# Handing the last rows of a row scan to the column scan tile to tile, with stores by quarter and loads on two queues

## The chip, the core and the metric

The kernel runs on one core of a Trainium2 chip. The metric is the device time of one execution in microseconds (us). Three executions of the kernel before took 4289.52, 4292.32 and 4297.63 us; the median is 4292.32.

## What is computed

Two layers run one after the other on a tensor of 32 images x 48 channels x 64 rows x 128 columns in float32. A layer normalizes its input by groups of three channels (`_gn`), runs four recurrences over the picture, and adds the result to its input. Each recurrence takes one row, or one column, after the other: the new one is the input plus a convolution of the one before (48 to 48 channels, 5 taps along the row or column, and a bias).

```python
def step(w, b):
    def f(carry, inp):
        nxt = inp + _conv1d(carry, w, b)
        return (nxt, nxt)
    return f
_, d_rest = jax.lax.scan(step(down_w, down_b), d0, xs[1:])     # down the 64 rows
_, u_rest = jax.lax.scan(step(down_w, down_b), u0, seq)        # and up again
_, r_rest = jax.lax.scan(step(right_w, right_b), r0, ws[1:])   # right over the 128 columns
_, l_rest = jax.lax.scan(step(left_w, left_b), l0, R[Ww - 2::-1])  # and left again
...
x = x + _L0_conv_ref(_gn(x), L0_conv_down_w, ...)
x = x + _L1_conv_ref(_gn(x), L1_conv_down_w, ...)
```

No step can begin before the one ahead of it has ended. The column scans need every row of the finished row scans.

## The kernel before

**Phases.** Images are taken in four groups of eight. `PHASES` (L104) lists twelve phases in their order: a `rows` phase scans one group down and up (126 steps), a `cols` phase scans a pair of groups right and left (254 steps). `scans` (L802) yields the steps; `step` (L728) is nine matmuls on TensorE (L741) and three additions on VectorE (L750), one for each of three blocks of 128 partitions, in the order 0, 2, 1.

**Layouts.** A row tile holds 384 partition rows (3 blocks `o` of 128): eight columns `e` of an octet times 48 channels. Its free axis runs over the row `h` and then over the 16 octets and the 8 images. `PIECES` (L51) says where the 48 channels of each `e` lie; channels of e = 2 and e = 5 straddle two blocks. A column tile is laid out the other way: `e` on the partitions is the row modulo 8, and the free axis runs over half (which group of the pair), octet of rows `a`, column modulo 8, octet of columns and image. The 128 columns are held by quarters of 32; a quarter is a third of the arena (`quarter`, L630), and the fourth takes the place of the first, which is spilled to DRAM (`spill_unit`).

**Going from rows to columns** is done through DRAM. `move_rows` (L589) stores rows of the row tile to the DRAM tensor `ups` in pieces of 128 bytes, ten DMAs for up to eight rows. `load_unit` (L633) loads one block of one half of a quarter, three or four DMAs.

**Order of work.** Work beside the scans is put on an agenda: `at(t, fn, ...)` (L820) runs `fn` when t steps have been written, and `in_order` (L235) chains all instructions of an engine in the order in which they were written. DMAs are issued from three queues: SP (`nc.sync`, the default of `dma`, L230), ACT (`nc.scalar`) and POOL (`nc.gpsimd`). A queue issues in order, so a DMA that waits holds up all that are behind it.

**The seam.** Twice a `cols` phase directly follows the `rows` phase of its second group (`follows`, L883): phase 2 after phase 1, and phase 6 after phase 5. There is no other work between, so the column scan must wait for the last rows. `plan_rows` (L853) stores the rows of the upward scan as they are finished, by eights (SP), but cuts the last eight in two: rows 2 to 7 when row 2 is done and rows 0 and 1 at the end. In `plan_cols` (L888) the second half of quarter 0 is loaded from POOL: rows 32 to 63, 16 to 31 and 8 to 15 ahead of the seam, then rows 2 to 7, and at the end rows 0 and 1. `hold_queues` (L648) puts a small DMA to the DRAM tensor `pin` on SP and a small copy on ACT, both reading what the first column step wrote. So the loads of quarter 1 behind them (L907; half 0 on SP, half 1 on ACT) start after that step. Quarter 2 (L910), the spill (L911) and quarter 3 (L912) follow on SP. During phase 2 SP also reads the rows of the next group (`plan_input`, L833): `take_in` loads them, ACT takes their statistics, POOL permutes them and SP stores them, each piece behind the one before.

Of the kernel before, what the change touches and what calls it, by code (L numbers as in the profile page):

```python
# [29 lines left out]
F32 = mybir.dt.float32  # L30
# [13 lines left out]
E8 = 8  # L44
FULL = 128
NG = E8 * C // FULL
NQ = 4
# [73 lines left out]
def kernel(  # L121
# [79 lines left out]
        dram.tile([2 * NG, FULL, UNIT], F32, tag=f"spill{i}", name=f"spill{i}")  # L201
        for i in range(4)
    ]
    pin = dram.tile([FULL, 1], F32, tag="pin", name="pin")


    HELD = (2, 1, 0)
# [3 lines left out]
        for half in range(2)  # L211
    }

    def by_row(t, e, h0, h1):


        t = t.rearrange("c (i q a e n) -> e a c i q n", i=E8, q=NQ, a=NH, e=E8)[e, h0 // E8]
        return t[:, h0 % E8 : h0 % E8 + h1 - h0].rearrange("c i q n -> c (i q) n")

    def lines(t, h0, h1):  # L220

# [8 lines left out]
    def dma(dst, src, queue=None):  # L230
        (queue or nc.sync).dma_start(dst, src)

    tail = {}

    def in_order(fn, *args):  # L235


        traced = nc.cur_bb.bb.instructions
        n = len(traced)
        fn(*args)  # L240
        for ins in traced[n:]:
            if ins.engine in tail:
                tc.add_manual_dep(
                    ins,
                    tail[ins.engine].name,
                    mybir.DependencyInfo(
                        mybir.DependencyClass.NoSync, mybir.DependencyReason.DATA
                    ),
                    reason="in_order",
                )  # L250
            tail[ins.engine] = ins

    def pieces(o):
# [332 lines left out]
    def row(k, h):  # L586
        return row_views(k)[h // HALF][:, :, h % HALF]

    def move_rows(k, h0, h1, to_dram):  # L589

        _, layer, g = PHASES[k]
        view = row_views(k)[h0 // HALF]
        t = (ups if to_dram else source)[layer][g]
        for h in range(h0, h1, E8):
            end = min(h1, h + E8)
            for o in range(NG):
                for e, c0, c1, p0 in pieces(o):
                    here = view[p0 : p0 + c1 - c0, o, h % HALF : h % HALF + end - h]
                    here = here.rearrange("p h (q n) -> p (h q) n", q=NQ)
                    there = by_row(t, e, h, end)[c0:c1]  # L600
                    if to_dram:
                        dma(there, here)
                    else:
                        dma(here, there)
# [25 lines left out]
    def quarter(k, j):  # L630
        return slot[slots(k)[j % 3]].rearrange("p (o s n) -> p s o n", s=2, o=NG)
# [13 lines left out]
                queue,  # L645
            )

    def hold_queues(k):  # L648

        done = quarter(k, 0)[:, 0, 0, RUN : RUN + 1]  # L650
        dma(pin, done)
        nc.scalar.copy(junk[:, BN - 1 :], done)

    def spill_unit(k, i, back):
        _, layer, pair = PHASES[k]
# [197 lines left out]
    def plan_rows(k, t0, prev):  # L853
        if k == 1:
            ahead, scaled = (-34, -18, -3, 12), (-12, -2, 17, 33)
        elif prev == "cols":
            ahead, scaled = (-28, -12, 4, 20), (-13, 3, 19, 35)
        else:
            ahead, scaled = (-54, -43, 0, 11), (-22, -8, 16, 30)
        if k:  # L860
            for i in range(4):
                at(t0 + ahead[i], move_rows, k, i * LOAD, (i + 1) * LOAD, False)
                at(t0 + scaled[i], scale_rows, k, i * LOAD, (i + 1) * LOAD)

        cuts = list(range(0, H + 1, E8))
        following = PHASES[k + 1][0] == "cols"
        if following and follows(k + 1):
            cuts = [0, E8 // 4] + cuts[1:]
        for h0, h1 in zip(cuts, cuts[1:]):
            t = t0 + 2 * (H - 1) - h0  # L870
            if k == 0:
                t += 16 if h0 >= HALF else 68
            elif not following:
                t = t0 + 92 + 5 * (H - h1) / E8 + (34 if h1 <= HALF else 0)
            at(t, move_rows, k, h0, h1, True)
        at(
            t0 + H - 1,
            nc.gpsimd.tensor_copy,
            last.rearrange("p (o n) -> p o n", o=NG),
            row(k, H - 1),  # L880
        )
# [6 lines left out]
    def plan_cols(k, t0, prev):  # L888
        _, layer, pair = PHASES[k]
        n = 2 * NG  # L890
        after = prev == "cols"
        if follows(k):
            at(t0 + 1.2, hold_queues, k)
        for i in range(n):
            if follows(k) and UNITS[i][1] == 1:
                other = nc.gpsimd
                at(t0 - 31 + i, load_unit, k, 0, i, 4, NH, 0, E8, other)
                at(t0 - 13 + i, load_unit, k, 0, i, 2, 4, 0, E8, other)
                at(t0 - 6 + i / n, load_unit, k, 0, i, 1, 2, 0, E8, other)
                at(t0 - 1.5, load_unit, k, 0, i, 0, 1, E8 // 4, E8, other)  # L900
                at(t0, load_unit, k, 0, i, 0, 1, 0, E8 // 4, other)
            else:
                early = 30 if after else 46 if k == 2 else 70
                at(t0 - early + 2 * i, load_unit, k, 0, i)
            if follows(k):
                queue = nc.scalar if i % 2 else nc.sync
                at(t0 + 1.5, load_unit, k, 1, i, 0, NH, 0, E8, queue)  # L907
            else:
                at(t0 + (3 if after else -24 + 2 * i), load_unit, k, 1, i)
            at(t0 + (38 if after else 8) + 2 * i, load_unit, k, 2, i)  # L910
            at(t0 + 33 + 2 * i, spill_unit, k, i, False)  # L911
            at(t0 + 50 + 2 * i, load_unit, k, 3, i)  # L912
        final = k == len(PHASES) - 1
        left = t0 + W - 1
        end = left + W - 1
        for i in range(n):

            t = left + 64 + 2 * i if layer == 0 else left + 39.5 + 4.5 * i
            at(t, spill_unit, k, i, True)
        units = []  # L920
        for n_done, j in enumerate((3, 2, 1, 0)):
            every = 4.5
            if j == 0 and PHASES[k + 1 if not final else k][0] == "rows":
                every = 7
            units += [(left + 34 + 32 * n_done + every * i, j, i) for i in range(n)]
        stats = None
        if layer == 0:
            stats = ResultStatsV(f"r{2 * pair}"), ResultStatsA(f"r{2 * pair + 1}")
        tiles = [stage[:, i] for i in range(4)]
        if layer:  # L930
            tiles += spare_tiles[0 : 2 if final else 1]
        n = len(tiles)
        direct = [u for u in units if not (final and u[1] == 0)]

        for u, (t, j, i) in enumerate(direct):
            nat = tiles[u % n]
            o, half = UNITS[i]
            if u < n:
                at(left + 16, load_residual, k, j, i, nat)
            if layer == 0:  # L940
                if u >= n:
                    at(direct[u - n][0] + 3, load_residual, k, j, i, nat)
                at(t, add_residual, k, j, i, nat)
                at(t + 4, keep_result, k, j, i)
                unit = quarter(k, j)[:, half, o]
                if half == 0:
                    for b in range(GB):
                        at(t + 5 + b, stats[0].take, j, o, unit, b)
                else:
                    at(t + 1, stats[1].take, j, o, unit)  # L950
            else:

                at(t, add_residual, k, j, i, nat)
                at(t + 2.5, permute_unit, k, j, i, nat, (nc.gpsimd, nc.scalar, nc.scalar))
                if final or j not in HELD:
                    at(t + 4.5, store_result, k, j, i, nat)
                else:
                    at(t + 4.5, hold_result, j, i, nat)
                if final and j == 1:
                    at(t + 4.7, load_residual, k, 0, i, last_tiles(k)[i])  # L960

                if u >= 2 and u - 2 + n < len(direct):
                    at(t + 4.6, load_residual, k, *direct[u - 2 + n][1:], tiles[(u - 2) % n])
        if layer == 0:
            t = units[-1][0] + 14
            g = 2 * pair
            spread(t, scaling(f"r{g}", 1, g, stats[0], r_masks, 8), 1)
            spread(t + 20, scaling(f"r{g + 1}", 1, g + 1, stats[1], r_masks, 8), 1)
        if layer:

            at(left + 10, nc.scalar.copy, junk[:, BN - 1 :], quarter(k, 3)[:, 0, 0, RUN - 1 : RUN])
        if layer and not final:
            todo = [(j, half, e) for j in HELD for half in range(2) for e in range(E8)]
            for n, what in enumerate(todo):
                at(end + 63 + 1.9 * n, let_result, *what)
        if final:
            at(end + 4, last_results, k)
# [231 lines left out]
```

## Time and profile before

| | before |
|---|---|
| median of three executions | 4292.32 us |
| the profiled execution | 4290.3 us |
| its span, first to last instruction | 4288.2 us |
| TensorE busy (matmuls) | 4058.9 us, 95% |
| VectorE busy | 2164.5 us, 50% |
| ScalarE busy | 1340.1 us, 31% |
| GpSimd busy | 886.2 us, 21% |
| granted TensorE clock, mean | 0.981 |
| DMA | 680.12 MB in 2,116,733 packets, 2,005,440 of them under 512 bytes |

Times in the trace count from the start of the span. In the lists of engines PE is TensorE, PEld its weight loads, DVE is VectorE, ACT ScalarE, POOL GpSimd and SP SyncE; "SPq" and "ACTq" are DMAs that these issue. `step_00r` is a step of layer 0, pair 0, right; `step_00d` and `step_00u` are layer 0, group 0, down and up. `arena<-upa` is a load from the DRAM tensor `ups` of layer 0, `upa<-arena` a store to it. "[14.10 <-DMA ...]" at the end of a line is how long the engine had been idle ahead of it and what ended that. fp32 matmuls show as two records each, so a step has 18 of them.

### The profile page before, as it was taken

To read this page: it belongs to the slowest core of one execution; us is meant where nothing else is said; L and a number is where in the kernel's file an instruction comes from. 1 tells how busy PE (TensorE), PEld (TensorE's weight loads), DVE (VectorE), ACT (ScalarE), POOL (GpSimd) and SP (SyncE) were. 2 spreads that over 40 slices of the span, in tenths; PEclk is the share of its full clock that TensorE was granted. 3 is DMA by queue.
4 is the path that set the end of the run, shared out by engine and by line. 5 is a ranking of instruction groups with operands and counts; after the bars stand their busy time and mean duration, and the time that the engine had idled before them with its cause. 6 is when DMAs were issued, how large, how long until landed. Compare 5 with 4: busy or idle time off the path is not lost. (4 is left out here: it accounts for less than half of the span.)

```text
span 4288.2 us, 89979 instructions
## 1 busy us (share of the span) xinstructions
PE 4058.9 (95%) x36648; PEld 4029.3 (94%) x36648; DVE 2164.5 (50%) x6503; ACT 1340.1 (31%) x2662; POOL 886.2 (21%) x906
## 2 busy tenths in 40 slices
PE   3699998999999999998999999999999999999992
PEld 1699998999999999998999999999999999999992
DVE  6345444446664444444446654444444444444443
ACT  1584301435793564100006772613000002210122
POOL 4271001325323020010005310000000024510352
PEclk9899999999999999999999999999999999999996
DMA  9599799857998979679308979939289049999999
GB/s 213 113 216 162 105 167 168 245 127 213 230 198 156 163 140 160 103 127 206 85 1 242 222 154 149 148 50 161 43 140 200 1 78 247 247 243 156 180 202 182
DMA packets 2116733, 680.12 MB, mean 159 GB/s; under 512 B 2005440, under 2 KB 2056160, under 8 KB 2076384
## 3 DMA queue, kind: packets, MB, share of 16 engines
q1 hardware_dynamic: 2015904, 581.64, 70.2%
q10 hardware_dynamic: 97216, 86.44, 9.9%
q0 software_dynamic: 3200, 6.30, 0.5%
q8 instruction: 288, 4.72, 0.5%
q14 instruction: 125, 1.02, 0.1%
HBM read 397.38 MB, written 295.98 MB: 162 GB/s over the span
## 5 line engine op out<-in xcount | busy, mean ns | idle before, releaser
L614 ACT ACTIVATE arena<-arena,offset,scale 128x256 f32<-128x256 f32 (+2 forms) x816 | 575.6, 801 | 432.9 <-DMA arena<-mid 176.1
L673 POOL TENSOR_TENSOR arena<-arena 128x2048 f32<-128x2048 f32 x80 | 363.1, 4553 | 1386.0 <-PE step_10l L741 434.1
L569 POOL COPY arena<-arena 96x256 f32<-96x256 f32 x448 | 265.0, 650 | 553.8 <-DMA arena<-in_x 444.2
L512 ACT ACTIVATE early<-arena 128x256 f32<-128x256 f32 x192 | 129.4, 674 | 477.2 <-POOL arena L673 471.2
L741 PE MATMUL step_00r<-arena,early 128*128 128x128 f32 x2286 | 251.5, 274 | 14.1 <-DMA arena<-upa 14.1
L741 PEld LDWEIGHTS step_00r<-arena,early 128*128 128x128 f32 x2286 | 251.1, 185 | 14.5 <-issue 14.4
L741 PE MATMUL step_01r<-arena,early 128*128 128x128 f32 x2286 | 250.6, 273 | 14.4 <-DMA arena<-upa 14.4
L741 PEld LDWEIGHTS step_01r<-arena,early 128*128 128x128 f32 x2286 | 250.4, 185 | 14.6 <-issue 14.5
L741 PE MATMUL step_11r<-arena,early 128*128 128x128 f32 x2286 | 251.3, 273 | 8.2 <-DVE arena L750 8.2
L741 PEld LDWEIGHTS step_11r<-arena,early 128*128 128x128 f32 x2286 | 250.8, 185 | 8.7 <-DVE arena L750 8.6
L741 PE MATMUL step_00l<-arena,wleft 128*128 128x128 f32 x2286 | 249.1, 272 | 0.0
L741 PEld LDWEIGHTS step_00l<-arena,wleft 128*128 128x128 f32 x2286 | 248.6, 184 | 0.0
L741 PE MATMUL step_10l<-arena,wleft 128*128 128x128 f32 x2286 | 248.5, 272 | 0.0
L741 PE MATMUL step_11l<-arena,wleft 128*128 128x128 f32 x2286 | 248.5, 272 | 0.0
L741 PE MATMUL step_01l<-arena,wleft 128*128 128x128 f32 x2286 | 248.4, 272 | 0.0
L741 PE MATMUL step_10r<-arena,early 128*128 128x128 f32 x2286 | 248.4, 272 | 0.0
L741 PEld LDWEIGHTS step_10l<-arena,wleft 128*128 128x128 f32 x2286 | 248.4, 184 | 0.0
L741 PEld LDWEIGHTS step_11l<-arena,wleft 128*128 128x128 f32 x2286 | 248.4, 184 | 0.0
L741 PEld LDWEIGHTS step_01l<-arena,wleft 128*128 128x128 f32 x2286 | 248.4, 184 | 0.0
L741 PEld LDWEIGHTS step_10r<-arena,early 128*128 128x128 f32 x2286 | 248.4, 184 | 0.0
L698 ACT COPY arena<-arena 128x256 f32<-128x256 f32 x172 | 99.7, 656 | 411.5 <-POOL arena L673 162.2
L240 ACT COPY early<-arena 128x1 f32<-128x1 f32 x2 | 0.4, 191 | 657.9 <-DVE arena L750 657.9
(189 smaller groups left out, 7171.3 us busy)
## 6 DMA issues: line engine op xcount, KB each, us to landing
arena<-in_x SPq DMA_DIRECT2D x24, 1536.0 KB, 11.6
xin<-arena SPq DMA_DIRECT2D x96, 384.0 KB, 4.7
arena<-xin SPq DMA_DIRECT2D x96, 384.0 KB, 8.5
mid<-arena SPq DMA_DIRECT2D x96, 384.0 KB, 7.8
arena<-mid SPq DMA_DIRECT2D x192, 192.0 KB, 4.2
upb<-arena SPq DMA_DIRECT2D x192, 192.0 KB, 3.9
arena<-upb SPq DMA_DIRECT2D x96, 384.0 KB, 12.3
arena<-xin SPq DMA_DIRECT2D x186, 192.0 KB, 4.3
```

Source lines behind the costliest of these rows:

```text
L240: fn(*args)
L512: nc.scalar.activation(junk[:, 0:n], view[:, b], AF.Identity, accum_out=self.sum[:, i, j : j + 1])
L569: copy(dst[:, r, q], src[:, r0 + r, q])
L614: nc.scalar.activation(args[0], args[0], AF.Identity, bias=args[2], scale=args[1])
L673: eng.tensor_tensor(unit, unit, nat, ALU.add)
L698: copy(by_w(perm)[:, a], src[:, a])
L741: nc.tensor.matmul(part(whole(ps[o])[0:m], -s), weights[:, i, at : at + m], part(src(i), s), start=seen[o] == 1, stop=seen[o] == left[o],)
```

## The change

- **Sends.** At a seam the last eight rows no longer go through DRAM for the first quarter of the columns. A new `send_row` copies a row piece by piece from the row tile straight into quarter 0 of the column tile: one DMA for each run of channels that is contiguous on both sides, at most 48 partitions x 128 bytes. For e = 0 to 3 of every octet of columns it is called as each row is finished (47 DMAs in all for rows 7 to 0). For e = 4 to 7, `send_rest` does all eight rows after the last one (47 more). The DMAs alternate between ACT and SP. `in_order` chains them across the two queues where they are written (the chain orders their scheduling; it adds no wait on the chip).
- **Removed loads and stores.** The stores of rows 2 to 7 and 0 to 1 ahead of the columns, and the POOL loads of those rows, are gone.
- **Stores by quarter.** Rows 8 to 15 are stored at row 8 for quarter 0 alone. Quarter 1 of rows 0 to 15 is stored after the last row, and quarters 2 and 3 of them a step or two later (SP; 20 DMAs for each quarter).
- **Quarter 1.** Its loads change sides: half 0 goes on ACT, half 1 on SP. On SP they stand between the stores of quarter 1 and those of quarters 2 and 3.
- **Hold.** `hold_queue` keeps only the copy on ACT. The DMA to `pin`, and `pin`, are gone.

```diff
-    pin = dram.tile([FULL, 1], F32, tag="pin", name="pin")
...
+            if ins.engine in queues and "DMA" in ins.opcode:
+                if fn in together and "queue" in tail:
+                    tc.add_manual_dep(
+                        ins,
+                        tail["queue"].name,
...
+                tail["queue"] = ins
...
-    def move_rows(k, h0, h1, to_dram):
+    def move_rows(k, h0, h1, to_dram, q=None):
...
-                    here = here.rearrange("p h (q n) -> p (h q) n", q=NQ)
-                    there = by_row(t, e, h, end)[c0:c1]
+                    there = by_row(t, e, h, end, q)[c0:c1]
+                    if q is None:
+                        here = here.rearrange("p h (q n) -> p (h q) n", q=NQ)
+                    else:
+                        here = here[:, :, q * RUN : (q + 1) * RUN]
...
-    def hold_queues(k):
-
-        done = quarter(k, 0)[:, 0, 0, RUN : RUN + 1]
-        dma(pin, done)
-        nc.scalar.copy(junk[:, BN - 1 :], done)
+    turns = [0]
+
+    def send_row(k, h, wanted):
+
+        here = row(k - 1, h)
+        for e, c0, c1, o, p0 in PIECES:
+            if e not in wanted:
+                continue
+            for i, d0, d1, to, q0 in PIECES:
+                a, b = max(c0, d0), min(c1, d1)
+                if i != h or a >= b:
+                    continue
+                turns[0] += 1
+                dma(
+                    quarter(k, 0)[q0 + a - d0 : q0 + b - d0, 1, to, e * RUN : (e + 1) * RUN],
+                    here[p0 + a - c0 : p0 + b - c0, o, 0:RUN],
+                    nc.scalar if turns[0] % 2 else nc.sync,
+                )
+
+    def send_rest(k, wanted):
+
+        for e in wanted:
+            for h in range(E8 - 1, -1, -1):
+                send_row(k, h, (e,))
+
+    together += [send_row, send_rest]
+
+    def hold_queue(k):
+
+        nc.scalar.copy(junk[:, BN - 1 :], quarter(k, 0)[:, 0, 0, RUN : RUN + 1])
...
-        if following and follows(k + 1):
-            cuts = [0, E8 // 4] + cuts[1:]
+        seam = following and follows(k + 1)
+        if seam:
+            cuts = cuts[2:]
+            end = t0 + 2 * (H - 1)
+            at(end - E8, move_rows, k, E8, 2 * E8, True, 0)
+            for h in range(E8 - 1, -1, -1):
+                at(end - h, send_row, k + 1, h, range(0, E8 // 2))
+            at(end, send_rest, k + 1, range(E8 // 2, E8))
+            for q in range(1, NQ):
+                at(end + 0.1 if q == 1 else end + 1.6, move_rows, k, 0, 2 * E8, True, q)
...
-            at(t0 + 1.2, hold_queues, k)
+            at(t0 + 1.2, hold_queue, k)
...
-                at(t0 - 1.5, load_unit, k, 0, i, 0, 1, E8 // 4, E8, other)
-                at(t0, load_unit, k, 0, i, 0, 1, 0, E8 // 4, other)
...
-                queue = nc.scalar if i % 2 else nc.sync
+                queue = nc.sync if UNITS[i][1] else nc.scalar
                 at(t0 + 1.5, load_unit, k, 1, i, 0, NH, 0, E8, queue)
```

More of the change, by code (lines that the diff above doesn't have):

```diff
@@ L212, with by_row @@
     }
-    def by_row(t, e, h0, h1):
+    def by_row(t, e, h0, h1, q):
         t = t.rearrange("c (i q a e n) -> e a c i q n", i=E8, q=NQ, a=NH, e=E8)[e, h0 // E8]
-        return t[:, h0 % E8 : h0 % E8 + h1 - h0].rearrange("c i q n -> c (i q) n")
+        t = t[:, h0 % E8 : h0 % E8 + h1 - h0]
+        return t.rearrange("c i q n -> c (i q) n") if q is None else t[:, :, q]
     def lines(t, h0, h1):
@@ L233 @@
     tail = {}
+    queues = (nc.sync.engine, nc.scalar.engine)
+    together = []
     def in_order(fn, *args):
@@ L250, in in_order @@
                 )
+            if ins.engine in queues and "DMA" in ins.opcode:
[3 more added lines that the diff above has]
+                        tail["queue"].name,
+                        mybir.DependencyInfo(
+                            mybir.DependencyClass.NoSync, mybir.DependencyReason.DATA
+                        ),
+                        reason="together",
+                    )
+                tail["queue"] = ins
             tail[ins.engine] = ins
@@ L646, in load_unit @@
             )
-    def hold_queues(k):
-        done = quarter(k, 0)[:, 0, 0, RUN : RUN + 1]
-        dma(pin, done)
-        nc.scalar.copy(junk[:, BN - 1 :], done)
+    turns = [0]
[13 more added lines that the diff above has]
+                    nc.scalar if turns[0] % 2 else nc.sync,
+                )
+    def send_rest(k, wanted):
[5 more added lines that the diff above has]
+        nc.scalar.copy(junk[:, BN - 1 :], quarter(k, 0)[:, 0, 0, RUN : RUN + 1])
     def spill_unit(k, i, back):
```

## The prediction

> **What bounds the kernel now.** I read the page first: TensorE (PE) is busy 95% of the span, so time is to be had only where PE stands still. The list of waits on PE comes next (columns: waited for, us in total, times, longest). Two of its lines belong to this change:
>
> ```profile
> PE step_01r L741 <- DMA arena<-upa: 14.4, 1, 14.4
> PE step_00r L741 <- DMA arena<-upa: 14.1, 1, 14.1
> ```
>
> Each is one stop, at the first column step of image pair 0 (call it seam 1) and of pair 1 (seam 2). Then the timeline of seam 1, all engines (start, duration, what, number of instructions, idle before):
>
> ```profile
> 649.34 4.94 POOL L231 DMA_DIRECT2D arena<-upa  x10 [11.26 <-DMA upa<-arena]
> 650.41 0.61 DVE L750 SCALAR_TENSOR_TENSOR arena<-step_01u,bd,early 128x128 f32<-128x128 f32 x2 [0.80 <-PE step_01u L741]
> 651.24 0.35 DVE L750 SCALAR_TENSOR_TENSOR arena<-step_01u,bd,early 128x128 f32<-128x128 f32 x1 [0.21 <-PE step_01u L741]
> 657.50 3.94 POOL L231 DMA_DIRECT2D arena<-upa  x8 [3.22 <-DMA upa<-arena]
> 662.19 1.00 POOL L231 DMA_DIRECT2D arena<-upa  x2 [0.74 <-issue]
> 665.29 6.88 PE L741 MATMUL step_00r<-arena,early 128*128 128x128 f32 x35 [14.10 <-DMA arena<-upa]
> ...
> 669.66 0.35 DVE L750 SCALAR_TENSOR_TENSOR arena<-step_00r,bd,arena 128x128 f32<-128x128 f32 x1 [0.76 <-PE step_00r L741]
> 671.43 0.61 DVE L750 SCALAR_TENSOR_TENSOR arena<-step_00r,bd,arena 128x128 f32<-128x128 f32 x2 [1.42 <-PE step_00r L741]
> 672.32 0.35 DVE L750 SCALAR_TENSOR_TENSOR arena<-step_00r,bd,arena 128x128 f32<-128x128 f32 x1 [0.28 <-PE step_00r L741]
> ```
>
> The last row is final at 651.59 (651.24 + 0.35). It is stored to DRAM by SP, POOL issues its loads until 663.19, and PE starts at 665.29. The loads at 649.34 are those of rows 8 to 15, whose stores SP had issued from 634.92 to 645.80.
>
> A seam costs more than its stop. DVE's third result of a step comes at 651.24, 669.66 and 672.32, against a pace of 1.975 us in rows and 1.955 in columns: 18.42 - 1.98 + 2.66 - 1.96 = **17.1 us**. At seam 2 the same results come at 1929.00, 1947.63 and 1949.63: 18.63 - 1.98 + 2.00 - 1.96 = **16.7 us**. Together 33.8 us, the most that this change can save there.
>
> **The skill beside the trace.** The Trainium skill, "TensorE: Matmul & The Clock Gate", Part 1, says that PE falls to half its clock after an idle window of about 3.4 us and recovers after a busy one. The trace agrees: the restart above holds 35 matmuls in 6.88 us (0.197 us each), where a busy stretch (672 to 690) has 167 in 18 us (0.108). So 17.1 - 14.1 = 3 us of seam 1 are a cold restart. I go by the trace for its size and by the page for this: a stop below 3.4 us need not bring it. The same skill, "DMA: Bandwidth & Descriptors", Specifications, says that transfers below 512 bytes are read, modified and written. The row bearing on it is `pin`, 128 writes of 4 bytes to DRAM, and what followed it (start:end, length, busy us and instructions of PE, PEld, DVE, ACT, POOL, then granted clock, DMA share, GB/s):
>
> ```profile
> 668.60:677.00 8.40, 8.40 (x69) 8.40 (x69) 3.54 (x11) 0.00 (x0) 0.00 (x0) 0.86 1.02 37
> 677.00:717.00 40.00, 39.98 (x369) 39.91 (x368) 19.66 (x62) 0.00 (x0) 0.00 (x0) 1.00 0.98 171
> ```
>
> DMA shows 102% busy at 37 GB/s, then 171. The same appears after the other `pin` (36 GB/s from 1946.5 to 1955, then 199) and nowhere else in the trace. That it is `pin` is a guess; I count its removal as 0 to 8 us earlier quarter loads, off PE's path.
>
> **The change, part by part.** *Sends.* Per seam, 94 DMAs of at most 6 KB go straight from row tile to column tile, 47 for columns e = 0 to 3 of each octet while the last eight rows are computed, 47 for e = 4 to 7 after the last row; SP and ACT take turns. They replace 10 stores on SP and 10 loads on POOL. No SBUF-to-SBUF DMA is in the trace. The nearest row has the same shape (48 partitions, one piece each):
>
> ```profile
> early<-taps SPq DMA_DIRECT2D x5, 6.0 KB, 1.7
> ...
> 480.11 14.28 SPq L231 DMA_DIRECT2D early<-taps  x25
> ```
>
> So 1.7 us from issue to landing, 0.57 us per issue on one queue (0.47 in its unbroken stretches). Upper bound: 2.5 us, as the 48 KB stores took in the busy seam; lower: 1.4.
>
> *The first column step* needs e = 0 of row 0, which DVE's first result of the last step completes at 650.76. Issue at once, landing 1.7 later, and about 0.6 from landing to matmul (POOL's last load was issued at 662.69, landed in 2.0, and PE began at 665.29): PE starts at 650.76 + 1.7 + 0.55 = 653.0, a stop of **1.8 us** from 651.19 instead of 14.1. Are the queues free by then? SP has 10 stores of rows 8 to 15, quarter 0 only, from 634.92. At 0.5 us each they end at 640; then 24 sends at 0.5 us, paced by rows arriving every 1.98 us, catch up by about 650. ACT has been idle for 184 us. POOL's loads of rows 8 to 15 can now go at 641.6 and end by 649.
>
> *The second 47*, 24 per queue, start at about 652.1. At 0.47 us the last goes at 662.9, at 0.57 at 665.2; with 1.7 and 0.55 they are usable at 665.2 to 667.5. Column e = 7 is added in step 7, at 653.0 + 6 x 1.955 + 1.2 = 665.9. So PE loses 0 to 1.6 us here; I take 1.0. In the program each send also waits for the eighth DMA before it, four back on its own queue: 4 x 0.47 = 1.9 just covers the landing, so a landing of 2.5 us means 0.63 per issue and 3 us lost. I add 0.5 us for a chance of a cold restart.
>
> A seam then costs 1.8 + 1.0 + 0.5 = 3.3 us. Saved: 33.8 - 2 x 3.3 = **27.2 us**.
>
> *Stores by quarter.* 60 stores (20 each of quarters 1, 2, 3; rows 0 to 15; 2.36 MB) move from before the seam to after the sends on SP. Their cover is the slack of the column loads behind them. Stores ran at 152 GB/s with DMA 94% busy (640 to 651): 5.2 us of DMA per quarter, and 0.5 us of SP for each.
>
> *Quarter 1* (6.29 MB) was issued from 668.8 to 703.9, the last part landing 12.8 us later at 716.7, for a use near 727. After: ACT starts half 0 at 663.2, once its sends are out (its tiny copy that waits for the first column step is then long free; SP no longer waits for that step). SP stores quarter 1 by about 675 and loads half 1 behind it; each load waits for these stores to land, and in the program the two queues share eight semaphores, so some stores wait for a load of ACT. 6.29 MB / 171 + 5.2 = 42 us: landed at 705 to 710. Use: 653.0 + 31 x 1.955 + 1.2 = 714.8. Covered by 5 to 10 us.
>
> *Quarters 2 and 3 stores*: 40, of which eight can queue behind quarter 1; 32 x 0.5 = 16 us, so 706 to 722. Then *quarter 2* with the next images' rows, 7.86 MB at 234 GB/s (717 to 750 before) = 34 us: 756, against a use at 777. Before, it ended at about 750.5. So SP runs 6 us later than before and PE 14 us earlier. *Quarter 3* hangs on the same queue, through rows of the next images, POOL's permuting and the spill: its last load was issued at 822.9 and landed by 832.2, for a use at 855.4. After: 838 for 841.4. Covered by 3 us only. At seam 2 no such rows are read, and quarter 3 had some 70 us. The removed POOL loads, the alternating halves and the removed `pin` free queues that nobody waits for: 0.
>
> Base: the profiled execution took 4290.3 us (span 4288.2, 2.1 around it), 2.0 below the median of the runs, 4292.3. From the profile 4263.1; on the median **4265**.
>
> **Rivals.** (1) *The sends are slower than the steps*: 0.75 us per send and queue. The last is usable at 652.1 + 23 x 0.75 + 2.25 = 671.6, 5.7 after its step, and the thin stretch keeps PE cold (+2.5): a seam costs 10, saved 13.8: 4278. For it: they are many and tiny, and each waits for a lane. Against: nothing in the trace of that size is over 0.57. (2) *The stop returns once, at column 96 or 32 of seam 1*: SP 15 us late instead of 6 makes quarter 3 wait 6 us, with a cold restart 8.5: 4273. For it: the 3 us of cover. Against: `pin`'s 8 us may come off. (3) *Slower*: the stores and quarter 1 block each other. If ACT's first loads take the 13 to 17 us that loads took at 669, the stores that share their semaphores wait so long, half 1 starts at 684 instead of 676, and at the 48 us that quarter 1 took before it lands at 732: a stop of 17 and 2.5 for the restart, 19.5 against 13.6 saved, at each seam: 4292.3 + 2 x 5.9 = 4304. It decides from a landing about 11 us after the use, at both seams. Against: at 669 both queues were full at once behind `pin`. (4) *It doesn't do what it says*: PE still waits for DRAM, for rows 8 to 15 as late as now (657): a seam costs about 8.3: 4275. Against: SP has only a quarter of them to store.
>
> **How the numbers follow.** Likeliest 4265, 0.58; (1) 0.17; (2) 0.14; (3) 0.08; (4) 0.03. The likeliest's own range is 4257 (a seam costs 0 to 1: hardly any stop, no restart) to 4271. The range goes to 4280, past (2), (4) and (1); beyond it lie (3) and some of (1), about 0.12, and little below 4256. Within 0.2% (8.6 us, about what a measurement of this kernel can tell from no change) means 4284 to 4301: the bad end of (1) and the mild end of (3), 0.07. Slower 0.08, faster 0.85.
>
> **What would show it.** Right: PE's two lines fall from 14 to about 2 us each; DVE's third results run on with one gap of about 4; the restart's matmuls are near 0.11 us; the sends land in under 2 us; no wait of PE on quarter loads near columns 32 and 96. Wrong: waits of DVE or PE on `arena<-arena` in steps 4 to 7 (1), on `arena<-upa` at column 32 at both seams (3) or at column 96 of seam 1 (2), or a first column step still released by POOL's loads (4).

## The result, and the profile after

| | before | after |
|---|---|---|
| median of 20 executions each, on one chip | 4292.05 us | **4299.45 us** |
| lowest and highest | 4278.85, 4299.49 | 4293.50, 4307.67 |
| ratio, after to before | | **1.0018**, 95% interval 1.0010 to 1.0025 |
| the profiled execution | 4290.3 us | 4306.0 us |
| its span | 4288.2 us | 4304.2 us |
| TensorE busy | 4058.9 us | 4068.6 us |
| granted TensorE clock, mean | 0.981 | 0.981 |

The changed kernel is slower by 7.4 us, where 27 us less were predicted. The profiled execution lies 6.6 us above the median of its kernel, and the one before 1.8 below its own, so the sums below, from profile to profile (+15.7 us), have 8.3 us more to explain than the medians do. In the changed kernel's listing the matmul is L782, VectorE's addition L791, ACT's scaling L630; a DMA is L231 still.

The list of waits on PE, after (us in total, times, longest):

```profile
PE step_00r L782 <- DVE arena L791: 10.3, 2, 9.3
...
PE step_01r L782 <- DMA arena<-arena: 6.2, 1, 6.2
PE step_00r L782 <- DMA arena<-arena: 6.0, 1, 6.0
PE step_01r L782 <- DVE arena L791: 4.2, 1, 4.2
```

The two stops of 14 us are gone, but four others stand in their place: about 6 us on the sends (`arena<-arena`) at the first column of both seams, 4.2 us a few columns later at seam 2, and 9.3 us (in the first line) somewhere in the first column scan. The timeline of seam 1 shows the first of them:

```profile
647.77 24.05 SPq L231 DMA_DIRECT2D arena<-arena  x36
648.10 24.72 ACTq L231 DMA_DIRECT2D arena<-arena  x36
...
651.05 0.35 DVE L791 SCALAR_TENSOR_TENSOR arena<-step_01u,bd,early 128x128 f32<-128x128 f32 x1 [0.21 <-PE step_01u L782]
...
657.02 16.53 PE L782 MATMUL step_00r<-arena,early 128*128 128x128 f32 x126 [6.01 <-DMA arena<-arena]
...
671.87 3.27 SPq L231 DMA_DIRECT2D upa<-arena  x6
```

Both queues issue sends almost without a pause until 672.8, 36 in 24.05 us on SP: 0.67 us each. VectorE has the last row by 651.40; PE starts at 657.02; SP's first store of quarter 1 comes at 671.87. PE's restart holds 126 matmuls in 16.53 us, 0.131 us each against 0.108 in a busy stretch: 2.9 us more. It is the cold clock, for over this stretch the granted clock was 0.84 (the number before the last two; the full clock is 1.00):

```profile
657.02:673.55 16.53, 16.53 (x126) 16.18 (x126) 5.86 (x18) 0.19 (x1) 0.00 (x0) 0.84 0.12 16
```

The 4.2 us at seam 2 belong to the last sends there. Four of them landed 3.8 to 5.0 us after their issue, where 1.76 was the median; the last landed at 1971.71, 0.53 us before PE went on. The stop of 9.3 us is at column 96:

```profile
858.33 0.61 DVE L791 SCALAR_TENSOR_TENSOR arena<-step_00r,bd,arena 128x128 f32<-128x128 f32 x2 [9.60 <-DMA xin<-arena]
858.73 3.49 PE L782 MATMUL step_00r<-arena,early 128*128 128x128 f32 x15 [9.29 <-DVE arena L791]
```

PE waits for VectorE, and VectorE for a DMA. The profile names `xin<-arena`, but that store was issued only at 849.63 and feeds no step. The last load of quarter 3 landed at 858.15, and VectorE's wait on that load's semaphore (the counter that tells of a landing) ended 0.04 us later, so that load is the releaser; `xin<-arena` landed only at 859.11 and after. Why it came so late is read from SP's queue, first after, then before:

```profile
671.87 15.61 SPq L231 DMA_DIRECT2D upa<-arena  x20
692.50 12.08 SPq L231 DMA_DIRECT2D arena<-upa  x10
704.92 27.26 SPq L231 DMA_DIRECT2D upa<-arena  x40
...
735.35 0.43 SPq L231 DMA_DIRECT2D arena<-in_x  x1
735.82 27.91 SPq L231 DMA_DIRECT2D arena<-upa  x17
...
821.85 25.31 SPq L231 DMA_DIRECT2D arena<-upa  x17
```

```profile
710.14 1.62 SPq L231 DMA_DIRECT2D arena<-in_x  x1
714.25 26.00 SPq L231 DMA_DIRECT2D arena<-upa  x17
...
796.62 26.60 SPq L231 DMA_DIRECT2D arena<-upa  x17
```

Of the 40 stores, six of the first eight waited for a load to land. The other 32 ran without a wait, 0.51 us apart in the median:

```profile
714.64 17.55 SPq L231 DMA_DIRECT2D upa<-arena  x32
```

The first read of the next images (`in_x`) is 25.2 us later than before, and everything behind it keeps that distance: the last 17 loads of quarter 3 begin 25.2 us later and the last one lands 25.9 us later (858.15 for 832.23).

**Where the time went.** VectorE's third result of each step, after minus before, gives the loss between any two steps. What a seam costs is the 17.1 or 16.7 us of the prediction plus the change of that difference across it.

| | predicted | profile after |
|---|---|---|
| seam 1 costs | 3.3 (gain 13.8) | 10.0 (gain 7.1): stops of 6.0 and 1.1, 2.9 of cold restart |
| column 96 of seam 1 | 0 | loss of 11.9: stop of 9.3, the rest cold |
| seam 2 costs | 3.3 (gain 13.4) | 14.7 (gain 2.0): stops of 6.2 and 4.2, and two cold restarts |
| steps 528 to 748, in the row scans behind the first column scan (1218 to 1679 us) | 0 | loss of 11.7 |
| all else | 0 | loss of 1.2 |
| sum | -27.2 | +15.7 |

On the medians forecast and result are 34.6 us apart (27.2 + 7.4). The two seams and column 96 make 6.7 + 11.4 + 11.9 = 30.0 of it.

### The profile page after: what moved, and what is told of

Same layout as the page of the kernel before. It is cut to its first block, busy times and chain, and to the rows that moved or that the text cites. A ratio compares the mean times of both kernels' runs of the same rounds, so it can differ in the third digit from the quotient of the medians.

```text
span 4304.2 us, 90375 instructions
## 1 busy us (share of the span) xinstructions
PE 4068.6 (95%) x36648; PEld 4037.7 (94%) x36648; DVE 2163.1 (50%) x6503; ACT 1340.3 (31%) x2662; POOL 881.4 (20%) x886
## 5 line engine op out<-in xcount | busy, mean ns | idle before, releaser
L630 ACT ACTIVATE arena<-arena,offset,scale 128x256 f32<-128x256 f32 (+2 forms) x816 | 575.9, 801 | 434.6 <-DVE arena L791 117.0
L782 PE MATMUL step_00r<-arena,early 128*128 128x128 f32 x2286 | 254.3, 275 | 16.4 <-DVE arena L791 10.3
L782 PEld LDWEIGHTS step_00r<-arena,early 128*128 128x128 f32 x2286 | 253.4, 187 | 17.3 <-DVE arena L791 11.0
L782 PE MATMUL step_01r<-arena,early 128*128 128x128 f32 x2286 | 252.6, 274 | 10.4 <-DMA arena<-arena 6.2
L782 PEld LDWEIGHTS step_01r<-arena,early 128*128 128x128 f32 x2286 | 252.0, 186 | 11.0 <-issue 6.5
L782 PE MATMUL step_11r<-arena,early 128*128 128x128 f32 x2286 | 252.1, 274 | 8.7 <-DVE arena L791 8.7
L782 PEld LDWEIGHTS step_11r<-arena,early 128*128 128x128 f32 x2286 | 251.6, 186 | 9.2 <-DVE arena L791 9.1
L782 PE MATMUL step_00l<-arena,wleft 128*128 128x128 f32 x2286 | 249.1, 272 | 0.0
L782 PE MATMUL step_10r<-arena,early 128*128 128x128 f32 x2286 | 248.7, 272 | 0.1
L782 PEld LDWEIGHTS step_10r<-arena,early 128*128 128x128 f32 x2286 | 248.5, 184 | 0.3 <-DVE arena L791 0.3
L782 PEld LDWEIGHTS step_00l<-arena,wleft 128*128 128x128 f32 x2286 | 248.6, 184 | 0.0
L782 PE MATMUL step_10l<-arena,wleft 128*128 128x128 f32 x2286 | 248.5, 272 | 0.0
L782 PE MATMUL step_11l<-arena,wleft 128*128 128x128 f32 x2286 | 248.5, 272 | 0.0
L782 PE MATMUL step_01l<-arena,wleft 128*128 128x128 f32 x2286 | 248.4, 272 | 0.0
L782 PEld LDWEIGHTS step_10l<-arena,wleft 128*128 128x128 f32 x2286 | 248.4, 184 | 0.0
L782 PEld LDWEIGHTS step_11l<-arena,wleft 128*128 128x128 f32 x2286 | 248.4, 184 | 0.0
L782 PEld LDWEIGHTS step_01l<-arena,wleft 128*128 128x128 f32 x2286 | 248.4, 184 | 0.0
L739 ACT COPY arena<-arena 128x256 f32<-128x256 f32 x172 | 99.5, 656 | 414.6 <-POOL arena L714 159.1
```

Of the source, the lines that this page charges most:

```text
L630: nc.scalar.activation(args[0], args[0], AF.Identity, bias=args[2], scale=args[1])
L739: copy(by_w(perm)[:, a], src[:, a])
L782: nc.tensor.matmul(part(whole(ps[o])[0:m], -s), weights[:, i, at : at + m], part(src(i), s), start=seen[o] == 1, stop=seen[o] == left[o],)
```

## Experiments

The theory after this reading: (a) a send takes about 0.64 us of its queue, so that 94 sends on two queues are slower than the steps; (b) the sends and the 60 small stores make SP late, and quarter 3 with it. The rivals are given with each run. In the table, seam costs and the loss at column 96 come from each profile as above; "rows between" is the loss over steps 528 to 748 against the first profile of before. These four columns tell of one execution: it lay 15.2 us under the median of its kernel with the stores from ACT, 10.4 under with whole stores, 8.7 under with three queues and stores from POOL, 12.4 above with three queues, and up to 6.6 away in the others.

| kernel | median us | ratio to before, 95% | seam 1 | col. 96 | seam 2 | rows between |
|---|---|---|---|---|---|---|
| before, beside these runs | 4291.9 to 4293.3 | 1 | 17.1 | 0 | 16.7 | 0 |
| before, second profile | one execution, 4283.6 | | 16.5 | 0 | 16.7 | 2.5 |
| after | 4299.45 | 1.0010 to 1.0025 | 10.0 | 11.9 | 14.7 | 11.7 |
| after, second profile | one execution, 4303.1 | | 9.9 | 14.3 | 13.4 | 8.7 |
| quarters 2, 3 stored from ACT | 4292.7 | 0.9988 to 1.0004 | 10.6 | 9.6 | 9.7 | 8.6 |
| quarters 2, 3 stored from POOL | 4285.5 | 0.9979 to 0.9993 | 11.3 | 0 | 14.9 | 6.4 |
| 20 whole stores for 60 | 4293.9 | 0.9995 to 1.0013 | 8.6 | 0 | 16.2 | 4.1 |
| sends on one queue | 4366.2 | 1.0150 to 1.0180 | 50.7 | 0 | 52.5 | 1.3 |
| sends on three queues | 4281.5 | 0.9954 to 0.9978 | 6.0 | 12.1 | 7.5 | 6.4 |
| three queues, stores from POOL | 4274.1 | 0.9944 to 0.9969 | 6.6 | 0.3 | 6.7 | 3.1 |
| the same, sends in order of need | **4270.2** | 0.9934 to 0.9961 | 3.7 | 0 | 5.0 | -2.0 |
| two queues, order of need, stores from POOL | 4288.0 | 0.9984 to 1.0005 | 12.4 | 0 | 13.5 | 1.4 |
| before without `pin` | 4308.5 | 1.0020 to 1.0044 | 23.7 | 0 | 24.6 | 4.5 |

**What a send costs: one queue instead of two.**

```diff
-                    nc.scalar if turns[0] % 2 else nc.sync,
+                    nc.scalar,
```

> The changed kernel with one edit: all sends on ACT's queue. Theory A (issue-bound per queue): about 0.60 us per send, the first column step begins near 668 instead of 657 and the last send lands near 697, so that the columns up to 8 follow the sends; a seam costs some 20 to 25 us more, less at seam 1 what column 96 would have waited anyway: 4325 to 4340. Rival B (a shared limit of 0.32 us per send): the sends end at 673 as with two queues, 4299.

Measured: 4366.2 us, worse than either said. The profile (ACT's queue):

```profile
643.25 74.59 ACTq L231 DMA_DIRECT2D arena<-arena  x94
```

The median distance from send to send is 0.643 us on this one queue, and it is 0.64 on each of two in the changed kernel. Rival B, a limit shared by the queues, is out: a second queue doubles the rate. The issue itself lasts 0.60 us in the median, whether it moves 16 partitions or 48. Another rival is the eight semaphores by which SP and ACT, in turn, learn of their landings: a DMA must wait until the one that last used its semaphore has landed. The traces rule it out for these two kernels. A send starts 0.8 us in the median after that landing with two queues and 2.5 us with one, so the wait was over before; the pace is the issue. The row scan of this execution ended 4.3 us later than in the profile after, so the 94 begin, seen from the rows, only 0.4 us later than there. They end at 717 instead of 697 since 93 x 0.643 is 60 us and 14 longer gaps add another 14. PE stops four times, for 43 us in all at seam 1.

**Three queues instead of two.**

```diff
-    queues = (nc.sync.engine, nc.scalar.engine)
+    queues = (nc.sync.engine, nc.scalar.engine, nc.gpsimd.engine)
...
-                    nc.scalar if turns[0] % 2 else nc.sync,
+                    (nc.sync, nc.scalar, nc.gpsimd)[turns[0] % 3],
```

> The changed kernel with one edit: the sends take turns on SP, ACT and POOL instead of SP and ACT. Theory A (the sends are bound by their issue on each queue, 0.64 us each): about 0.22 us per send over all, the stop at the first column step falls from 6.0 to 2 or 3 us at both seams and the second stop of seam 2 (4.2 us) goes. What seam 1 gains is lost again at column 96, where SP's late quarter 3 decides, unless SP is also earlier, by up to 8 us with 16 sends less; so 4284 to 4292. Rival B (the sends are bound by something that all queues share, such as DMA engines or landings): the period per queue rises to about 0.95 us, stops unchanged, 4299.

Measured: 4281.5 us. The last send is issued at 663.2 instead of 672.2, with 0.66 to 0.70 us from send to send on SP and ACT and 0.495 on POOL. The first stop falls to 4.3 us (seam 1) and 5.4 us (seam 2), not to 2 or 3; the second ones go. Column 96 still costs 12.1, as expected: SP reads the next images at 724.7 instead of 735.4, and quarter 3 lands at 854.0, while PE is 4 us earlier. Rival B's 0.95 us is out and Theory A holds: the three paces together make a send every 0.20 us. But on SP and ACT the issue is no longer the limit. It lasts only 0.55 us here, a send lands after 2.8 us (1.76 with two queues), and at seam 1 it starts 0.07 us in the median after the landing that it must wait for. So these two queues now run against their eight semaphores, four sends back on each (2.8 / 4 = 0.70 us). The Trainium skill, "DMA: Bandwidth & Descriptors", section "Issuing engines are not separate DMA queues", says that several issuers save only the time to initiate a DMA, "which is usually small relative to the DMA itself". For these sends it is not small: with two queues 0.60 us of issue stand against a landing of 1.76, and 47 x 0.64 = 30 us of each queue set the pace.

**SP's backlog, first lever: the stores of quarters 2 and 3 on ACT.** `move_rows` takes a queue for its stores; the call becomes

```diff
-                at(end + 0.1 if q == 1 else end + 1.6, move_rows, k, 0, 2 * E8, True, q)
+                at(end + 0.1 if q == 1 else end + 1.6, move_rows, k, 0, 2 * E8, True, q, None if q == 1 else nc.scalar)
```

> The changed kernel with one edit: the 40 stores of quarters 2 and 3 of the last sixteen rows go on ACT's queue, behind its loads of quarter 1, and no longer on SP's. Theory A (SP's backlog of stores made quarter 3 late): SP starts quarter 2 at about 715 instead of 732, the last load of quarter 3 lands about 17 us earlier, near 841, and the stop of 9.3 us at column 96 of seam 1 goes with its cold restart. About 12 us less than the changed kernel: 4287. Rival B (quarter 3 is late through the bytes moved, or through the chain of the next images' rows, not through SP's queue): the stop stays at 6 us or more, 4296 to 4300.

Measured: 4292.7 us, between the two, and inconclusive. The lever did not move what it should. ACT needed from 684.0 to 721.1 for the 40 stores, in between SP's loads, and SP read the next images at 723.0 in an execution whose row scan ended 10.3 us earlier than in the profile after: a gain of 2 us, not 17. The trace shows why. Of SP's 13 loads from 683.9 on, eight start within 0.1 us of the landing of the DMA that had last used their semaphore, and in five of the eight that is a store on ACT; the first load of quarter 2 then waits another 8.3 us on semaphores that ACT's stores use. The stores left SP's queue, but SP still waited for them. What is lower in this profile is mostly seam 2, whose second stop is missing: its last sends landed after 1.8 us, where in both profiles after the last ones took 3.8 to 5.0. What delays them there is not shown.

**Second lever: the same stores on POOL,** which has semaphores of its own (the same diff with `nc.gpsimd`).

> The changed kernel with one edit: the 40 stores of quarters 2 and 3 of the last sixteen rows go on POOL's queue, which has semaphores of its own, and no longer on SP's. Put on ACT they still took 38 us, between SP's loads, and SP was only 4 us earlier, so that run settled little. Theory A (SP's backlog makes quarter 3 late): SP goes from its loads of quarter 1 straight to quarter 2, at about 705 instead of 732; quarter 3's last load lands near 835; no stop at column 96; about 12 us less than the changed kernel: 4287. Rival B (quarter 3 hangs on something else): the stop of 8 us stays, 4296 to 4300. POOL's stores run beside the second half of the sends and beside quarter 1, which may cost a few us there.

Measured: 4285.5 us, 14.0 less than after. POOL's queue, then SP's:

```profile
650.30 23.85 POOL L231 DMA_DIRECT2D upa<-arena  x40 [3.80 <-DVE arena L791]
```

```profile
672.97 13.43 SPq L231 DMA_DIRECT2D upa<-arena  x20
691.18 17.41 SPq L231 DMA_DIRECT2D arena<-upa  x13
710.70 0.33 SPq L231 DMA_DIRECT2D arena<-in_x  x1
...
798.15 27.42 SPq L231 DMA_DIRECT2D arena<-upa  x17
```

The 40 stores take 23.9 us there, 0.62 apart in the median. SP is back at 710.7 (710.14 before), quarter 3 lands at 836.9, and there is no stop at column 96. Theory A holds and B falls: the late quarter 3 is SP's backlog. The seams gain nothing, 11.3 and 14.9.

**Third lever: 20 stores of whole rows in place of 60 by quarter.**

```diff
-            for q in range(1, NQ):
-                at(end + 0.1 if q == 1 else end + 1.6, move_rows, k, 0, 2 * E8, True, q)
+            at(end + 0.1, move_rows, k, 0, 2 * E8, True)
```

> The changed kernel with one edit: in place of the 60 stores by quarter after the seam, 20 stores of whole rows 0 to 15 (the first quarter is stored again with them: 3.1 MB instead of 2.4). Theory A (the number of stores on SP makes quarter 3 late): SP is done with them at about 693 and starts quarter 2 near 712 instead of 732; no stop at column 96 (12 us less), but half 1 of quarter 1 starts 5 to 8 us later and may stop PE at column 32 by up to 8 us: 4287 to 4295. Rival B: the stop at column 96 stays, 4299 or more.

Measured: 4293.9 us. A third of the stores with a third more bytes: SP reads the next images at 716.7, quarter 3 lands at 847.2, just in time. Half 1 of quarter 1 is later, and column 32 of seam 1 stops PE for 1.7 us. The two levers agree in the profiles, though this one is of an execution 10.4 us under its median, and with quarter 3 only just in time it does not show that the median execution was spared at column 96.

**Both faults mended, then the order of the sends.** Three queues and the POOL stores together:

> Two edits together: the sends on three queues (which gave 4281) and the stores of quarters 2 and 3 on POOL behind its sends (663 to 683). Theory A: what is left in the three-queue version is the stop at column 96 (9.0 us and a restart); it goes: about 4270. Rival C (the POOL stores collide with quarter 1): quarter 1 lands after its use at about 718 and PE stops at column 32, by 5 to 15 us at both seams: 4280 to 4295.

Measured: 4274.1 us. Column 96 is gone (0.3), quarter 1 was in time, the seams cost 6.6 and 6.7. Then the order of need on top:

```diff
-                at(end - h, send_row, k + 1, h, range(0, E8 // 2))
-            at(end, send_rest, k + 1, range(E8 // 2, E8))
+                at(end - h, send_row, k + 1, h, range(0, E8 // 2 if h > 2 else 2 if h else 1))
+            at(end, send_rest, k + 1, range(1, E8))
...
-                send_row(k, h, (e,))
+                if e >= (E8 // 2 if h > 2 else 2 if h else 1):
+                    send_row(k, h, (e,))
```

> The version of the run before with one more edit: the sends are ordered by when they are needed. Rows 2 and 1 send only columns e = 0 and 1 as they are finished, row 0 only e = 0, and all the others follow by column from e = 1. Theory A (the 4 to 5 us stop that three queues leave is a queue of less urgent sends ahead of row 0): the stop falls to about 2 us at each seam, 4 to 5 us less over all: 4265. Rival D (the stop is the way from the last sum to the landing, or the total number of sends decides): no change, 4270, or the stop comes back in the columns after the first.

Measured: 4270.2 us, the best of all, 0.52% under before (0.39 to 0.66%). The 4.0 us under the version without the order are of the size that Theory A said, but the intervals of the two overlap; what speaks for the order is the stops. The timeline of its seam 1 (its listing has the matmul at L783):

```profile
649.46 20.53 ACTq L231 DMA_DIRECT2D arena<-arena  x25
...
649.85 19.22 SPq L231 DMA_DIRECT2D arena<-arena  x24
651.68 13.81 POOL L231 DMA_DIRECT2D arena<-arena  x28
656.57 10.43 PE L783 MATMUL step_00r<-arena,early 128*128 128x128 f32 x90 [1.43 <-DMA arena<-arena]
665.48 9.60 POOL L231 DMA_DIRECT2D upa<-arena  x16
667.64 4.21 PE L783 MATMUL step_00r<-arena,early 128*128 128x128 f32 x36 [0.64 <-DVE arena L792]
...
672.46 3.77 PE L783 MATMUL step_00r<-arena,early 128*128 128x128 f32 x32 [0.61 <-DVE arena L792]
```

The stop is 1.43 us (3.95 in the version without the order) where 1.8 had been predicted for the changed kernel. The restart takes 0.116 us a matmul at a granted clock of 1.00, so it is not cold, and two stops of 0.6 follow. At seam 2 PE stops once, for 3.3 us. The gains, 13.4 and 11.7, are the sum that the prediction had made, 27.2, less two; the medians differ by 21.7.

**Is it the order alone?** The same order on two queues, with the POOL stores:

> The version with the stores of quarters 2 and 3 on POOL (4285), the sends on SP and ACT as in the changed kernel, but in the order of need (rows 2 and 1 first send only e = 0 and 1, row 0 only e = 0, all others by column). Theory A (94 sends at 0.64 us on two queues are the limit, whatever their order): PE starts at about 654 instead of 657, but the sends still end near 672, and what the first stop gains comes back as stops in the columns 1 to 7: 4284 to 4287. Rival D (the order is what costs): both stops shrink and stay small, 4 us less at each seam: 4277.

Measured: 4288.0 us, no better than the 4285.5 without it. PE starts at 653.8 after a stop of 4.5, and the time comes back in stops of 3.4, 1.1 and 1.0 before 676: the seam costs 12.4, not 11.3 (seam 2: 13.5, not 14.9). So the number of sends on two queues is the limit, and the order showed a gain only with the third queue.

**`pin`.** Before, without the DMA to `pin`:

```diff
-    pin = dram.tile([FULL, 1], F32, tag="pin", name="pin")
...
-        dma(pin, done)
```

> The kernel before with one edit: the small DMA to pin is left out, the copy on ACT stays (SP's loads of quarter 1 then start as soon as SP reaches them). Theory A (the 128 writes of 4 bytes are what slows the loads behind them): no stretch of DMA fully busy at 37 GB/s after the first column step; quarter 1 lands about 8 us earlier; the time stays at 4292 within 4 us, since PE does not wait for it. Rival B (the slow stretch comes from two queues full of loads at once): the stretch stays.

Measured: 4308.5 us, 15.2 slower than before. Both theories missed that. Stretches of this profile (columns as in the prediction; the last two are DMA share and GB/s), then its timeline (its matmul is L739, its DMA L230):

```profile
660.00:673.00 13.00, 0.05 (x1) 0.08 (x1) 0.00 (x0) 0.00 (x0) 2.84 (x6) 0.50 1.02 193
673.00:681.00 8.00, 8.00 (x56) 7.85 (x57) 2.63 (x8) 0.19 (x1) 0.00 (x0) 0.77 1.03 193
```

```profile
659.96 15.45 SPq L230 DMA_DIRECT2D arena<-upa  x11
672.95 3.26 PE L739 MATMUL step_00r<-arena,early 128*128 128x128 f32 x13 [21.77 <-DMA arena<-upa]
```

The guess about the writes was right: with no `pin` there is no stretch at 37 GB/s. Rival B is out, for with SP and ACT both loading, from 681 to 720, it is 207 GB/s. But the same DMA had been a gate. Without it SP starts quarter 1 at 659.96, while POOL still loads the last two rows of quarter 0; those land at 672.4 instead of 664.7, and PE stops for 21.8 us instead of 14.1. In the changed kernel the gate isn't missed, for its sends and stores keep SP away from quarter 1 until 692.

**The rows between the seams.** In steps 528 to 748 VectorE waits for ACT's scaling and ACT for SP's loads. VectorE's waits for ACT between 1200 and 1670, after, and then before, differ by 12.1 us, about the loss of 11.7:

```profile
DVE arena L791 <- ACT arena L630: 14.7, 6, 4.6
```

```profile
DVE arena L750 <- ACT arena L614: 2.6, 3, 1.1
```

SP's order of instructions there is the same in both kernels, and it issues almost without a pause from 1095 to 1515. After, it was 4.9 us behind before at 1050, as PE was, 8.9 at 1110 and about 16 at 1470. In every profile of the table SP and PE are equally far from before at 1050, within 0.2 us: SP's lateness at the seam has been made up by then and is not carried into these scans. Is the loss due to the change or to the execution? Both kernels were profiled again, unedited.

> The kernel before, with no edit, profiled once more. In the row scans between the two seams (steps 528 to 748, the end of the first column scan and the two row scans that follow) the profile after lost 11.7 us against the profile before, though the change edits nothing there, and the other profiles taken since lost 2 to 9 us there, one of them (without pin) of a kernel that is the same as before in these scans. Theory E (that stretch varies from execution to execution): this profile also stands 2 to 9 us above the first one of before over those steps. Rival F (the change makes these scans slower): it agrees with the first profile within 1.5 us.

> The changed kernel, with no edit, profiled once more. Theory E (the row scans between the seams vary from execution to execution): over steps 528 to 748 it differs from the first profile of the changed kernel by 3 us or more. Rival F: again 10 to 13 us above before. In either case the three stops of the first profile return, since they follow from the queues: about 6 us at both seams and 9 us at column 96 of seam 1, and the whole lies between 4293 and 4308.

Measured: before 2.5 us, after 8.7. The three stops returned (6.6, 5.4 and 11.7 us). So this stretch does vary, by 2.5 and 3.0 us between two profiles of one kernel, as Theory E had said if only just, and Rival F's numbers came neither time. Versions that hold the whole change lost from -2.0 to 8.6 there. But the two profiles after have the highest losses of all, and the before-like ones 0, 2.5 and 4.5. The medians leave little for it: seams and column 96 make +2.8 us of the 7.4 after, so 4.6 remain for all else, where 0.7 to 3.6 remain in the other kernels but two (9 with whole stores, -3.6 with three queues; their profiles lie 10.4 and 12.4 us off their medians). A small part of the loss may belong to the change; no run shows a way by which it would come about, and the question stays open.

## Why the prediction was wrong

- **What bounds the kernel, and what a seam costs (17.1 and 16.7): right.** The best version took 13.4 and 11.7 of it.
- **The price of a send: the first term that failed.** I took 0.47 to 0.57 us from `early<-taps`, a load from DRAM, as the nearest row; a send takes 0.64. The landing of 1.7 us was right (1.76 in the median), but for the last four sends of seam 2 with 3.8 to 5.0, which brought the second stop there. "Catch up by about 650" failed with it: six sends a row at 0.32 us (two queues) are 1.9 us against 1.98 for a row, so a queue that starts behind stays behind. The send of row 0, e = 0 was ready at 650.57 and issued at 654.88, behind 13 less urgent ones on the two queues; it landed at 656.57 and PE went on at 657.02. Stop 6.0, not 1.8.
- **The cold restart: 0.5 us a seam predicted, 2.9 and 4.4 measured.** After the stops of 6.0 and 6.2 us the granted clock was 0.84 and 0.88 over the next 126 matmuls, after the stop of 1.4 in the best version 1.00. That agrees with the Trainium skill, "TensorE: Matmul & The Clock Gate", Part 1, by which an idle window of about 3.4 us halves the clock. Only 0.5 us had been put down for the restart because the stop was to be 1.8; once a stop is long enough for it, the error in the stop grows by half (6.0 + 2.9).
- **SP's lateness: the second term that failed, and by my own numbers.** I had the stores of quarters 2 and 3 end at 722, against a start of quarter 2 near 710 before; that is 12 us. I wrote 6, since I gave the block of loads 34 us (717 to 750) where it had taken 41 before (710 to 750.55). With 12, quarter 3 lands at 844 for a use at 841: the cover of 3 us was gone on paper. On the chip SP was 25.2 us late at `in_x`: 11.9 are those of my numbers; 8.3 more since the sends ended 8 us later and quarter 1 landed at 714.3 instead of 706; 1.9 since the 32 stores behind that landing ended 17.9 us after it and not 16; and 3.1 for three loads of quarter 2 that stand ahead of `in_x` and that the 710 includes. The 0.5 us a store was right. From `in_x` to the last landing of quarter 3 it is 122.1 us before and 122.8 after: lateness at the one end comes out whole at the other.
- **Quarter 1: right in kind.** Landed at 714.3 instead of 705 to 710; PE, itself late, needed it after 714.8 and did not stop.
- **The rivals.** (1) and (2) both came true. I had set them side by side with chances of their own, 0.17 and 0.14, as if one excluded the other. They share a cause: slow sends hold SP, SP's stores start late, and quarter 3 follows; the 11.9 us of my own numbers come on top. Rival (1)'s seam of 10 was met at seam 1 and passed at seam 2; (2) cost 11.9, not 8.5. The two together, with both seams as in (1), are 4278 + 8.5 = 4286.5, which the prediction itself counted as no change. (3), the slower one, did not happen: no stop at column 32. (4) did not happen either.
- **`pin`: the guess about the writes was right, but not the reading that nobody waits for it.** It was a gate as well, worth 6.6 and 7.9 us a seam in the kernel before. In the changed kernel its removal shows no cost, but no run put it back there.
- **The rows between the seams: not foreseen,** 6 to 12 us between profiles of the two kernels, about 4.6 of it in the medians if one profile of the seams stands for its kernel; cause open.

## What to carry over

Count the issues before the bytes: many tiny DMAs cost a fixed time of their queue each, so set number times that time, over the queues, against the steps that must hide them, and start from the backlog that is there when they begin. Carry the lateness of a queue to the last thing that hangs on it, with the block lengths of the trace itself; a cover of 3 us is no cover. Rivals that feed each other get one chance together, and their times are added.

## What the runs showed of the hardware

- A DMA from SBUF to SBUF occupied SP or ACT for 0.60 us and came every 0.64, alike for 16, 32 and 48 partitions of 128 bytes and with one or two queues in use. Loads of `early<-taps` took 0.42 us of SP and came every 0.47. The stores behind the sends took SP 0.47 and came every 0.51, though most of them carry 48 KB and a send 6 KB at most.
- On POOL the same sends came every 0.495 us, but the stores every 0.62: it was the quicker queue for the one and the slower for the other. The same 40 stores took 23.9 us from POOL, 27.3 from SP, where six of the first eight waited for loads to land, and 37.1 from ACT, among SP's loads.
- With sends on three queues a landing took 2.8 us in the median on SP and ACT, 1.76 on two queues.
- 128 writes of 4 bytes to DRAM held the loads beside them at 37 GB/s for 8.4 us; without them 193 GB/s in the same place.
